# Attention block: query and key biases moved into the projection weights, and VectorE's work of a unit put in another order

## The chip, the cores and the metric

The kernel runs on one NeuronCore of a Trainium2 chip. Five engines work side by side, each on its own queue and in that queue's order: TensorE (PE in the profile; its weight loads are shown as PEld), VectorE (DVE), ScalarE (ACT), GpSimd (POOL), and SyncE (SP), which here only starts DMA transfers. The metric is the device time of one execution in microseconds (us). Before the change three runs took 2816.67, 2817.36 and 2818.38 us; the median is 2817.36 us.

## The reference, cut to what matters

Four sequences of 1024 tokens with 512 features go through a layer norm, a two-branch attention with 16 heads of 128, and a small fp8-rounded product, all added to the input.

```python
xn = _layernorm(x)                                   # mean 0 over the 512 features
q  = apply_rope(rmsnorm(xn @ Wq  + bq,  qn_w), pos)  # 16 heads x 128
lk = apply_rope(rmsnorm(xn @ Wlk + blk, kn_w), pos)
lv = xn @ Wlv + blv
# branch 1: top 8 of the compressed keys (one entry for every 4 tokens)
# branch 2: softmax over a window of the previous and the current 128 tokens
out = merged @ Wo + bo
```

The two lines with `bq` and `blk` are what the change is about. Since `xn` has mean zero over the features, subtracting one and the same row from every row of a weight matrix leaves `xn @ W` as it is. With the first row subtracted, the first row of the new matrix is zero: feature 0 then contributes nothing, and its place can carry a bias, if the input's feature 0 is replaced by 1.

## The kernel before, in words

The work is cut into 32 chunks of 128 tokens (`t`, eight for each of four sequences; `c` is the chunk's place in its sequence) and, within a chunk, into eight units of two heads (`u`), so 256 units `n = 8 t + u`. One long loop (line 791) runs over `s`; in one pass it issues parts of several units, so that the stages of different units overlap. What each engine does in which order is exactly the order of the calls in this loop; nothing reorders it later.

In one pass before the change, for `8 <= s`:

1. `scores(s)` (TensorE, L572 to L583), `keep_context(s-2)` (ScalarE), `weigh(s)` (VectorE L605 to L611: mask, maximum, top 8; ScalarE: the exponentials, L612 and L620), `queries(s+3)` (TensorE, L445 and L446), `settle(s)` (VectorE L627 to L638: sums, reciprocals, scaling).
2. one step of the chunk's preparation, then `squares(s+3)` (ScalarE, L296) and `spread(s+3)` (GpSimd, L290 and L291: the reciprocal root `r`), `settle_window(s)` (ScalarE, L643), `to_output(s-2)` (TensorE, L753), another step.
3. `turn(s)` (VectorE transposes the probabilities, L661; SP writes them to DRAM, L669), `values_of(s+1)` (TensorE, L537), `normalize(s+3)` (VectorE L467 and, in `rotate`, GpSimd L309 beside VectorE L310, then VectorE L311 and L312, which wait for L309), `values(s-1)` (TensorE, L720), `fetch(s)` (SP reads the probabilities back, L703), `turn_keys(s+3)` and `fetch_keys(s+3)` (VectorE L512 and L515; SP L520 and L530), `keep_values(s+1)` (ScalarE).

In the first chunk the turned keys and probabilities don't go through DRAM: TensorE transposes them (`turn_keys_here`, L490; `turn_here`, L684) and ScalarE and VectorE copy the results (`keep_keys`, `keep_turned`). In the first four units VectorE and GpSimd also round a weight matrix (`round_w2`, by `quantize`, L262 to L273).

`queries` makes 128 x 512 products: four float32 matmuls over the 512 features and a fifth, L446, which adds the bias: its weights are a column of `sel` repeated, its moving operand `bias_b`, three bfloat16 pieces of the bias.

`chunk_prep` is a generator that prepares a chunk two chunks ahead in steps ("A0", "B0", ...), two steps a pass: statistics (L329), the normalised rows `xn` (L337, VectorE), their transposes (L342), the copy `xnT` (L345, ScalarE), the compressed keys and values. For the first chunk it runs at once, at the start.

PSUM tiles: `qp` and `sc` have two buffers each, `pp` (transposes, `vp` and the chunk's products) has two, `ctx` one.

Of the kernel before, what the change touches and what calls it, by code (L numbers as in the profile page):

```python
# [23 lines left out]
HALF = ROPE // 2  # L24
# [14 lines left out]
def kernel(  # L39
# [46 lines left out]
    def scratch(name, shape=(P, 512), dtype=F32):  # L86
        return work.tile(list(shape), dtype, tag="scratch", name=name, bufs=2)
# [8 lines left out]
    x_tiles, angles = {}, {}  # L96
# [148 lines left out]
    def late_constants():  # L245
# [6 lines left out]
        nc.tensor.transpose(bp[:, 0:NH], blv_n, ident[:NH, :NH])  # L252
        nc.scalar.activation(blvT, bp[:, 0:NH], AF.Copy, scale=0.5)

    def quantize(dst, src, scalar, tag, m=None):

        v = scratch(f"qv_{tag}") if tag[0] == "x" else src
        if m is None:  # L260
            m = scratch(f"qm_{tag}")
        nc.vector.tensor_scalar(v, src, scalar, None, ALU.mult)  # L262
        nc.vector.tensor_scalar(
            m.bitcast(U32), v.bitcast(U32), 0x7F800000, None, ALU.bitwise_and
        )
        nc.vector.tensor_scalar(m, m, FP8_MIN_NORMAL, 1.5 * 2.0**20, ALU.max, ALU.mult)
        nc.gpsimd.tensor_tensor(v, v, m, ALU.add)
        yield
        nc.gpsimd.tensor_tensor(v, v, m, ALU.subtract)
# [3 lines left out]
        nc.gpsimd.tensor_tensor(dst, v, m, ALU.add)  # L273
        yield
# [22 lines left out]

    def rotate(th, cs, nh, a, name):

        p = th.shape[0]  # L300
        a = a.rearrange("p (h t f) -> p h t f", h=nh, t=2)
        bb = work.tile([P, 4, 2, HALF], F32, tag="ropeb", name=f"rb_{name}", bufs=1)
        bb = bb[:p, 0:nh]
        x12 = th[:, :, 0:ROPE].rearrange("p h (t f) -> p h t f", t=2)

        def wide(v):
            return v.unsqueeze(1).unsqueeze(1).to_broadcast([p, nh, 2, HALF])

        nc.gpsimd.tensor_tensor(bb, x12, wide(cs[:, HALF:ROPE]), ALU.mult)  # L309
        nc.vector.tensor_tensor(a, x12, wide(cs[:, 0:HALF]), ALU.mult)  # L310
        nc.vector.tensor_tensor(x12[:, :, 0, :], a[:, :, 0, :], bb[:, :, 1, :], ALU.subtract)  # L311
        nc.vector.tensor_tensor(x12[:, :, 1, :], a[:, :, 1, :], bb[:, :, 0, :], ALU.add)  # L312

# [4 lines left out]
    def chunk_prep(t):  # L318
# [14 lines left out]
        if c == 0:  # L333
            nc.gpsimd.memset(cv, 0.0)
        yield "B0"
        xn = scratch(f"xn_{t}")
        nc.vector.tensor_scalar(xn, xt, st[:, 6:7], r, ALU.subtract, ALU.mult)  # L337
        yield "A1"
        yield "B1"
        xp = pp(f"xp_{t}")  # L340
        for k in range(KK):
            nc.tensor.transpose(xp[:, ts(k, P)], xn[:, ts(k, P)], ident)  # L342
        yield "A2"
        xnT = work.tile([P, KK, P], F32, tag="xnT", name=f"xnT_{t}")
# [55 lines left out]
        er = rstd_of(ess, 1, 1.0 / D, EPS_RMS, f"er_{t}")  # L400
        ck = kv[:, 0:1, :]
        yield "A6"
        yield "B6"
        nc.vector.scalar_tensor_tensor(
            ck[:, 0, :], ck[:, 0, :], er, norm_w[0:NE, 1, :], ALU.mult, ALU.mult
        )
        ra = work.tile([NE, ROPE], F32, tag="ra_e", name=f"ra_e{t}", bufs=1)
        rotate(ck, angles[t][1], 1, ra, f"e{t}")
        yield "A7"
        yield "B7"  # L410
        cp = pp(f"cp_{t}")
        nc.tensor.transpose(cp[:, 0:NE], ck[:, 0, :], ident[:NE, :NE])
        yield "A8"
        nc.vector.tensor_copy(ckT[:, ts(c, NE)], cp[:, 0:NE])  # L414
        yield "B8"

    def chunk_eight(t):

        xt, xnT = x_tiles["sum", t], chunks[t]
        x8 = work.tile([P, KK * P], BF16, tag="x8", name=f"x8_{t}", bufs=1)  # L420
        src = xnT.rearrange("p k s -> p (k s)")
# [14 lines left out]
    def place(n):  # L436

        return divmod(n, NU)

    def queries(n):  # L440
        t, u = place(n)
        xnT = chunks[t]
        qp = psum.tile([P, 512], F32, tag="qp", name=f"qp_{n}")
        for k in range(KK):
            nc.tensor.matmul(qp, xnT[:, k, :], wqk_sb[u][:, k, :], start=(k == 0), stop=False)  # L445
        nc.tensor.matmul(  # L446
            qp, sel[:, u : u + 1].to_broadcast([P, P]), bias_b, start=False, stop=True
        )
# [10 lines left out]
        w["r"] = rstd_of(w["ss"], 4, 1.0 / D, EPS_RMS, f"r_{n}")  # L459

    def normalize(n):
        t, u = place(n)
        w = units[n]
        qp, r = w.pop("qp"), w["r"]
        th = work.tile([P, 4, D], F32, tag="th", name=f"th_{n}", bufs=1)
        for i in range(4):
            nc.vector.scalar_tensor_tensor(  # L467
                th[:, i, :],
                qp[:, ts(i, D)],
                r[:, i : i + 1],  # L470
                norm_w[:, i // 2, :],
                ALU.mult,
                ALU.mult,
            )
        thb = work.tile([P, NB, 2, 2 * BLK], F32, tag="thb", name=f"thb_{n}", bufs=1)
        spare = thb.rearrange("p b t x -> p (b t x)")[:, 0 : 4 * ROPE]
        rotate(th, angles[t][0], 4, spare, f"{n}")
        w["th"], w["thb"] = th, thb

    def by_dma(n):  # L480

        return NU <= n < NN - 1
# [308 lines left out]
    for s in range(-3, NN + 2):  # L791
        t, u = place(s)

        if s == -2 or u == 7 and 0 <= t and t + 2 < NT:
            running = [*running[-2:], chunk_prep(t + 2)]
        if u == 3 and 0 <= t < NT:
            load_x(t, "sum")
        if u == 6 and 0 <= t < NT:
            running = [*running[-2:], chunk_eight(t)]
        if u == 4 and 0 <= t and t + 2 < NT:  # L800
            load_x(t + 2, "norm")

        for_unit(s, (scores, 0), (scores, 1))
        for_unit(s - 2, (keep_context,))
        for_unit(s, (weigh, 0), (weigh, 1))
        for_unit(s + 3, (queries,))
        if s + 2 < NU:
            for_unit(s + 2, (turn_keys_here,))
        for_unit(s, (settle, 0), (settle, 1))
        if s < 0:  # L810
            until(first, ("B3", "B4", "B6")[s + 3])
        steps()
        for_unit(s + 3, (squares, (0, 1, 2, 3)), (spread,))
        if s + 2 < NU:
            for_unit(s + 2, (keep_keys,))
        for_unit(s, (settle_window, 0), (settle_window, 1))
        for_unit(s - 2, (to_output,))
        steps()
        if by_dma(s):
            turn(s)  # L820
        if s == -1:
            until(first, "B7")
        for_unit(s + 1, (values_of,))
        if s == -1:
            until(first, "B8")
        if not by_dma(s):
            for_unit(s, (turn_here,))
        for_unit(s + 3, (normalize,))
        for_unit(s - 1, (values,))
        if by_dma(s):  # L830
            fetch(s)
        else:
            for_unit(s, (keep_turned,))
        if s + 3 >= NU:
            for_unit(s + 3, (turn_keys,), (fetch_keys,))
        for_unit(s + 1, (keep_values,))
        if s < NU:
# [63 lines left out]
```

## Time and profile before

| | before |
|---|---|
| median of three runs | 2817.36 us |
| the profiled execution | 2818.54 us |
| its span | 2816.8 us |
| granted TensorE clock | 0.998 |
| TensorE busy | 2779.5 us |
| VectorE busy | 2244.6 us |
| ScalarE busy | 1282.1 us |
| GpSimd busy | 815.2 us |
| L446 (the bias matmul) | 256 times, 97.0 us busy |

The span runs from the first to the last instruction of one profiled execution. Busy time is the time in which an engine had at least one instruction in it. Matmuls are pipelined: the next one starts while the last is still draining, so the time from one start to the next, and not the mean duration of a row, is what a matmul takes from TensorE.

### The profile page before, as it was taken

Reading aid. Unit: us, or ns where it says so; the run is one execution under the profiler, and the core shown is the slowest. Engines: PE = TensorE matmul, PEld = TensorE weight load, DVE = VectorE, ACT = ScalarE, POOL = GpSimd, SP = SyncE. Lnnn points to the kernel's source line nnn. Section 1 sums busy time; section 2 is a strip of 40 time slices with the busy share of each in tenths; the row PEclk is TensorE's granted clock in tenths of the full one; section 3 lists DMA queues with packets and bytes.
Section 4 is the critical chain, followed back from the end, with each engine's and each line's share of the span. In section 5 each row is a group of like instructions: output and inputs, shape, how many; then the busy total and the mean of one; then the engine's idle time right before and its main releaser. Section 6 shows DMA issues by size and latency. Waiting matters only on the chain.

```text
span 2816.8 us, 48762 instructions
## 1 busy us (share of the span) xinstructions
PE 2779.5 (99%) x12969; PEld 1873.5 (67%) x12969; DVE 2244.6 (80%) x9132; ACT 1282.1 (46%) x5075; POOL 815.2 (29%) x1161
## 2 busy tenths in 40 slices
PE   6999999999999999999999999999999999999998
PEld 4666666666666666666666666666666666666665
DVE  5777888888777788888877777888887777788886
ACT  3445444444444444444444444444444444444443
POOL 3432222222333222322233333223222332322221
PEclk9999999999999999999999999999999999999999
DMA  7345455555445455555544454555554454455554
GB/s 231 91 136 141 134 143 150 148 154 150 130 124 139 137 140 144 148 152 149 155 127 127 134 136 134 154 150 148 145 154 121 134 134 135 133 158 156 145 145 114
DMA packets 620852, 399.85 MB, mean 142 GB/s; under 512 B 306881, under 2 KB 573985, under 8 KB 620577
## 3 DMA queue, kind: packets, MB, share of 16 engines
q1 hardware_dynamic: 608352, 383.18, 49.3%
q10 hardware_dynamic: 12224, 13.56, 1.6%
q8 instruction: 105, 1.72, 0.3%
q14 instruction: 171, 1.39, 0.2%
HBM read 212.53 MB, written 184.03 MB: 141 GB/s over the span
## 4 chain that ended last, share of the span: by engine, by line
PE 92%; DVE 3%; DMA 1%; POOL 1%; ACT 1%; SPq 0%; issue 0%; ACTq 0%; DVEq 0%; POOLq 0%
PE qp L445 30%; PE op L753 15%; PE vp L537 15%; PE cp L720 13%; PE sc L582 5%; PE sc L572 4%; PE sc L579 4%; PE qp L446 2%; PE yp L352 2%; PE fp L425 1%; DMA pr<-probB 1%; PE ep L382 1%; PE xp L342 0%; DMA probT<-pr 0%; ACT junk L296 0%
## 5 line engine op out<-in xcount | busy, mean ns | idle before, releaser
L445 PE MATMUL qp<-wqk,xnT 128*128 128x512 f32 x2048 | 944.6, 604 | 4.6 <-DMA scales<-in_L_ffn_scale_dram 3.3
L612 ACT ACTIVATE prob<-sc,neg 128x256 f32<-128x256 f32 (+1 forms) x512 | 236.1, 461 | 1029.6 <-DVE taken L611 975.9
L445 PEld LDWEIGHTS qp<-wqk,xnT 128*128 128x128 f32 x2048 | 370.3, 191 | 384.2 <-issue 370.5
L537 PEld LDWEIGHTS vp<-wlv,xnT 128*128 128x128 f32 x2048 | 388.8, 190 | 166.9 <-issue 113.1
L537 PE MATMUL vp<-wlv,xnT 128*128 128x256 f32 x2048 | 484.2, 379 | 4.8 <-DVE lkT L497 3.0
L753 PE MATMUL op<-wo,cT 128*128 128x512 f32 x1024 | 488.0, 599 | 0.5 <-ACT cT L735 0.5
L467 DVE SCALAR_TENSOR_TENSOR th<-qp,r,norm_w 128x128 f32<-128x128 f32 x1024 | 283.2, 339 | 104.8 <-POOL r L291 104.8
L661 DVE STREAM_TRANSPOSE probB<-prob 128x512 f32<-128x512 f32 (+2 forms) x494 | 283.1, 611 | 92.8 <-ACT prob L643 81.5
L290 POOL TENSOR_SCALAR r<-ss 128x4 f32<-128x4 f32 x256 | 49.9, 195 | 1038.5 <-ACT junk L296 1032.9
L309 POOL TENSOR_TENSOR rb<-th,cs 128x256 f32<-128x256 f32 x256 | 245.3, 958 | 269.4 <-DVE th L467 268.3
L296 ACT ACTIVATE junk<-qp 128x128 bf16<-128x128 f32 x1024 | 284.2, 278 | 54.8 <-PE qp L446 26.5
L720 PE MATMUL cp<-probT,lv 128*128 128x128 f32 x1920 | 299.3, 276 | 6.6 <-DMA probT<-pr 6.5
L753 PEld LDWEIGHTS op<-wo,cT 128*128 128x128 f32 x1024 | 186.4, 190 | 177.9 <-issue 120.5
L720 PEld LDWEIGHTS cp<-probT,lv 128*128 128x128 f32 x1920 | 274.4, 192 | 23.3 <-issue 10.0
L291 POOL TENSOR_TENSOR r<-r,nhalf 128x4 f32<-128x4 f32 x256 | 259.2, 1012 | 21.4
L720 PE MATMUL cp<-probT,cv 128*128 128x128 f32 x1536 | 256.1, 276 | 0.0
L582 PE MATMUL sc<-ckT,qT 128*128 128x96 f32 (+7 forms) x1024 | 227.1, 304 | 0.7 <-DVE ckT L414 0.7
L643 ACT ACTIVATE prob<-prob,tot 128x256 f32<-128x256 f32 (+1 forms) x512 | 223.2, 484 | 3.2 <-DVE tot L637 3.2
L549 ACT COPY lv<-vp 128x256 f32<-128x256 f32 x256 | 94.9, 371 | 276.2 <-PE cp L720 241.6
L720 PEld LDWEIGHTS cp<-probT,cv 128*128 128x128 f32 x1536 | 213.5, 193 | 0.0
L311 DVE TENSOR_TENSOR th<-thb,rb 128x128 f32<-128x128 f32 x256 | 87.2, 341 | 155.7 <-POOL rb L309 155.0
L605 DVE CUSTOM_DVE_ANT_0 sc<-sc,mask_b 128x256 f32<-128x256 f32 (+1 forms) x512 | 202.8, 396 | 8.3 <-PE sc L583 7.7
(123 smaller groups left out, 4054.0 us busy)
## 6 DMA issues: line engine op xcount, KB each, us to landing
pr<-probB SPq DMA_DIRECT2D x127, 512.0 KB, 3.0
probT<-pr SPq DMA_DIRECT2D x508, 128.0 KB, 2.9
qk<-thb SPq DMA_DIRECT2D x992, 64.0 KB, 2.0
pr<-probB SPq DMA_DIRECT2D x96, 384.0 KB, 2.8
probT<-pr SPq DMA_DIRECT2D x384, 96.0 KB, 2.4
qT<-qk SPq DMA_DIRECT2D x248, 128.0 KB, 2.3
lkT<-qk SPq DMA_DIRECT2D x248, 128.0 KB, 2.6
x_norm<-_attn_hidden_states_dram SPq DMA_DIRECT2D x32, 256.0 KB, 3.3
```

The source lines that it names most:

```text
L291: nc.gpsimd.tensor_tensor(r, r, nhalf[: ss.shape[0], 0:n], ALU.pow)
L296: nc.scalar.activation(junk[: src.shape[0]], src, AF.Square, accum_out=acc)
L309: nc.gpsimd.tensor_tensor(bb, x12, wide(cs[:, HALF:ROPE]), ALU.mult)
L445: nc.tensor.matmul(qp, xnT[:, k, :], wqk_sb[u][:, k, :], start=(k == 0), stop=False)
L467: nc.vector.scalar_tensor_tensor(th[:, i, :], qp[:, ts(i, D)], r[:, i : i + 1], norm_w[:, i // 2, :], ALU.mult, ALU.mult,)
L537: nc.tensor.matmul(vp[:, 0:256], xnT[:, k, :], wlv_sb[u][:, k, :], start=(k == 0), stop=(k == KK - 1),)
L582: nc.tensor.matmul(sc[:, spa], q, ckT[:, 0:m], start=True, stop=False)
L612: nc.scalar.activation(prob[:, loc], sc[:, loc], AF.Exp, bias=neg[:, 0:1], scale=-1.0, accum_out=tot[:, 0:1],)
L643: nc.scalar.mul(prob[:, loc], prob[:, loc], tot[:, 0:1])
L661: nc.vector.transpose(pb[:, :, ds(h * g, g), :], prob[:, parts[0] * P : (parts[-1] + 1) * P].rearrange("p (g b i) -> p b g i", b=NB, i=BLK),)
L720: nc.tensor.matmul(blocks(cp[:, h, :]), v, probT[:, :, h * len(parts) + i - parts[0], :], start=(i == parts[0]), stop=(i == parts[-1]),)
L753: nc.tensor.matmul(op, cT[:, h, :], wo_sb[u][:, h, :], start=(u == 0 and h == 0), stop=(u == NU - 1 and h == 1),)
```

## The change

- **Bias.** From the second chunk on, L446 is left out. Instead `xnT` has a fifth block of 128 features: a copy of the first block with its first row set to 1 (one more ScalarE copy and a VectorE memset for each chunk but the first), and `queries` uses this block in place of the first. The weights for it are made during the first chunk: in pass `s` (0 to 7) VectorE subtracts the first row from all of `wqk[s]` (128 x 2048 float32 elements), and SP's queue then writes the two bias pieces over its first row. The row comes to all partitions by two DMAs on SP's queue, one pass ahead. The first chunk itself still uses L446.
- **Mean.** So that `xn` has a mean of zero to rounding, the mean is taken out twice: GpSimd negates it, ScalarE subtracts it in place and sums the result, GpSimd scales that sum, and VectorE's `xn` subtracts the rest. `xn` comes one step later in `chunk_prep`; two of the later steps are joined, so that the generator has one pair of steps less.
- **Order.** `settle_window(s)` comes ahead of `squares(s+3)` on ScalarE. VectorE's `normalize` runs in pass `s` for unit `s+2` instead of `s+3`, ahead of `turn(s)`; its last two operations (`end_rotation`) come after `turn(s)` and the chunk's steps; `turn_keys(s+2)` follows there, so its four DMAs stand ahead of `fetch(s)` on SP's queue, and `fetch_keys(s+2)` behind it. In the first chunk `turn_keys_here` and `keep_keys` work on unit `s+1` instead of `s+2`. `rotate`'s GpSimd product has a buffer of its own for the units and one for the compressed keys.

```diff
+    def load_first_row(u):
+        row = work.tile([P, 1024], F32, tag="probB", name=f"first_row_{u}", bufs=1)[:, 0:512]
+        for i, w in enumerate((Wq, Wlk)):
+            nc.sync.dma_start(row[:, ts(i, 256)], w[0, ts(u, 256)].partition_broadcast(P))
+        first_row[u] = row
+    def fold_first_row(u):
+        w = wqk_sb[u]
+        nc.vector.tensor_tensor(
+            w, w, first_row.pop(u).unsqueeze(1).to_broadcast([P, KK, 512]), ALU.subtract
+        )
+        for i, bias in enumerate((bq, blk)):
+            nc.sync.dma_start(
+                w[0:1, 0, ts(i, 256)], bias[ts(u, 256)].partition_broadcast(1)
+            )
...
         nc.vector.tensor_tensor(a, x12, wide(cs[:, 0:HALF]), ALU.mult)
+        yield
         nc.vector.tensor_tensor(x12[:, :, 0, :], a[:, :, 0, :], bb[:, :, 1, :], ALU.subtract)
...
+        nc.gpsimd.tensor_scalar(off[:, 0:1], st[:, 6:7], -1.0, None, ALU.mult)
+        nc.scalar.activation(
+            xt, xt, AF.Identity, bias=off[:, 0:1], scale=1.0, accum_out=off[:, 1:2]
+        )
+        nc.gpsimd.tensor_scalar(off[:, 1:2], off[:, 1:2], 1.0 / HID, None, ALU.mult)
...
-        nc.vector.tensor_scalar(xn, xt, st[:, 6:7], r, ALU.subtract, ALU.mult)
+        nc.vector.tensor_scalar(xn, xt, off[:, 1:2], r, ALU.subtract, ALU.mult)
...
+        if t:
+            nc.scalar.copy(xnT[:, KK, :], xp[:, 0:P])
+            nc.vector.memset(xnT[0:1, KK, :], 1.0)
...
         for k in range(KK):
-            nc.tensor.matmul(qp, xnT[:, k, :], wqk_sb[u][:, k, :], start=(k == 0), stop=False)
-        nc.tensor.matmul(
-            qp, sel[:, u : u + 1].to_broadcast([P, P]), bias_b, start=False, stop=True
-        )
+            nc.tensor.matmul(
+                qp,
+                xnT[:, k if k or not t else KK, :],
+                wqk_sb[u][:, k, :],
+                start=(k == 0),
+                stop=(t > 0 and k == KK - 1),
+            )
+        if not t:
+            nc.tensor.matmul(
+                qp, sel[:, u : u + 1].to_broadcast([P, P]), bias_b, start=False, stop=True
+            )
...
         for_unit(s + 3, (queries,))
-        if s + 2 < NU:
-            for_unit(s + 2, (turn_keys_here,))
+        if s + 1 < NU:
+            for_unit(s + 1, (turn_keys_here,))
         for_unit(s, (settle, 0), (settle, 1))
+        for_unit(s, (settle_window, 0), (settle_window, 1))
+        for_unit(s + 2, (normalize,))
+        if by_dma(s):
+            turn(s)
...
         for_unit(s + 3, (squares, (0, 1, 2, 3)), (spread,))
...
         steps()
-        if by_dma(s):
-            turn(s)
+        for_unit(s + 2, (end_rotation,))
+        if s + 2 >= NU:
+            for_unit(s + 2, (turn_keys,))
...
-        for_unit(s + 3, (normalize,))
         for_unit(s - 1, (values,))
         if by_dma(s):
             fetch(s)
...
-        if s + 3 >= NU:
-            for_unit(s + 3, (turn_keys,), (fetch_keys,))
+        if s + 2 >= NU:
+            for_unit(s + 2, (fetch_keys,))
         for_unit(s + 1, (keep_values,))
+        if 0 <= s < NU:
+            fold_first_row(s)
+        if 0 <= s + 1 < NU:
+            load_first_row(s + 1)
```

More of the change, by code (lines that the diff above doesn't have):

```diff
@@ L253, in late_constants @@
         nc.scalar.activation(blvT, bp[:, 0:NH], AF.Copy, scale=0.5)
+    first_row = {}
+    def load_first_row(u):
[12 more added lines that the diff above has]
+            )
     def quantize(dst, src, scalar, tag, m=None):
@@ L301, in rotate @@
         a = a.rearrange("p (h t f) -> p h t f", h=nh, t=2)
-        bb = work.tile([P, 4, 2, HALF], F32, tag="ropeb", name=f"rb_{name}", bufs=1)
-        bb = bb[:p, 0:nh]
+        bb = work.tile([p, nh, 2, HALF], F32, tag=f"ropeb{nh}", name=f"rb_{name}", bufs=1)
         x12 = th[:, :, 0:ROPE].rearrange("p h (t f) -> p h t f", t=2)
@@ L335, in chunk_prep @@
         yield "B0"
+        off = work.tile([P, 2], F32, tag="off", name=f"off_{t}")
+        nc.gpsimd.tensor_scalar(off[:, 0:1], st[:, 6:7], -1.0, None, ALU.mult)
[3 more added lines that the diff above has]
+        nc.gpsimd.tensor_scalar(off[:, 1:2], off[:, 1:2], 1.0 / HID, None, ALU.mult)
+        yield "A1"
         xn = scratch(f"xn_{t}")
-        nc.vector.tensor_scalar(xn, xt, st[:, 6:7], r, ALU.subtract, ALU.mult)
-        yield "A1"
+        nc.vector.tensor_scalar(xn, xt, off[:, 1:2], r, ALU.subtract, ALU.mult)
         yield "B1"
@@ L343, in chunk_prep @@
         yield "A2"
-        xnT = work.tile([P, KK, P], F32, tag="xnT", name=f"xnT_{t}")
-        nc.scalar.copy(xnT.rearrange("p k s -> p (k s)"), xp)
+        xnT = work.tile([P, KK + 1, P], F32, tag="xnT", name=f"xnT_{t}")
+        nc.scalar.copy(xnT[:, 0:KK, :].rearrange("p k s -> p (k s)"), xp)
+        if t:
+            nc.scalar.copy(xnT[:, KK, :], xp[:, 0:P])
+            nc.vector.memset(xnT[0:1, KK, :], 1.0)
         chunks[t] = xnT
@@ L402, in chunk_prep @@
         yield "A6"
-        yield "B6"
         nc.vector.scalar_tensor_tensor(
@@ L407, in chunk_prep @@
         ra = work.tile([NE, ROPE], F32, tag="ra_e", name=f"ra_e{t}", bufs=1)
-        rotate(ck, angles[t][1], 1, ra, f"e{t}")
-        yield "A7"
-        yield "B7"
+        for _ in rotate(ck, angles[t][1], 1, ra, f"e{t}"):
+            pass
+        yield "B6"
         cp = pp(f"cp_{t}")
         nc.tensor.transpose(cp[:, 0:NE], ck[:, 0, :], ident[:NE, :NE])
-        yield "A8"
+        yield "A7"
         nc.vector.tensor_copy(ckT[:, ts(c, NE)], cp[:, 0:NE])
-        yield "B8"
+        yield "B7"
     def chunk_eight(t):
@@ L420, in chunk_eight @@
         x8 = work.tile([P, KK * P], BF16, tag="x8", name=f"x8_{t}", bufs=1)
-        src = xnT.rearrange("p k s -> p (k s)")
+        src = xnT[:, 0:KK, :].rearrange("p k s -> p (k s)")
         yield from quantize(x8, src, scales[:, 0:1], f"x_{t}")
@@ L461, in normalize @@
     def normalize(n):
-        t, u = place(n)
         w = units[n]
@@ L476, in normalize, with end_rotation @@
         spare = thb.rearrange("p b t x -> p (b t x)")[:, 0 : 4 * ROPE]
-        rotate(th, angles[t][0], 4, spare, f"{n}")
+        w["rotation"] = rotate(th, angles[place(n)[0]][0], 4, spare, f"{n}")
+        next(w["rotation"])
         w["th"], w["thb"] = th, thb
+    def end_rotation(n):
+        for _ in units[n].pop("rotation"):
+            pass
     def by_dma(n):
@@ L813 @@
         for_unit(s + 3, (squares, (0, 1, 2, 3)), (spread,))
-        if s + 2 < NU:
-            for_unit(s + 2, (keep_keys,))
-        for_unit(s, (settle_window, 0), (settle_window, 1))
+        if s + 1 < NU:
+            for_unit(s + 1, (keep_keys,))
         for_unit(s - 2, (to_output,))
         steps()
-        if by_dma(s):
-            turn(s)
+        for_unit(s + 2, (end_rotation,))
+        if s + 2 >= NU:
+            for_unit(s + 2, (turn_keys,))
         if s == -1:
@@ L823 @@
         for_unit(s + 1, (values_of,))
-        if s == -1:
-            until(first, "B8")
         if not by_dma(s):
             for_unit(s, (turn_here,))
-        for_unit(s + 3, (normalize,))
         for_unit(s - 1, (values,))
```

## The prediction, written before the result

> **What bounds the kernel.** I read the page's head first: who is busy, and what the chain that ended last consists of.
>
> ```profile
> span 2816.8 us, 48762 instructions
> ...
> PE 2779.5 (99%) x12969; PEld 1873.5 (67%) x12969; DVE 2244.6 (80%) x9132; ACT 1282.1 (46%) x5075; POOL 815.2 (29%) x1161
> ...
> PE 92%; DVE 3%; DMA 1%; POOL 1%; ACT 1%; SPq 0%; issue 0%; ACTq 0%; DVEq 0%; POOLq 0%
> ```
>
> TensorE is busy 99% and makes 92% of the chain. A busy share can hide waits, so I checked it in the timeline of TensorE for one unit of a late chunk (columns: start, length, engine, line, operation).
>
> ```profile
> 1405.55 3.68 PE L445 MATMUL qp<-wqk,xnT 128*128 128x512 f32 x8
> 1409.07 0.38 PE L446 MATMUL qp<-bias_b,sel 128*128 128x512 bf16 x1
> 1409.28 1.88 PE L753 MATMUL op<-wo,cT 128*128 128x512 f32 x4
> 1411.00 1.89 PE L537 MATMUL vp<-wlv,xnT 128*128 128x256 f32 x8
> 1412.73 0.61 PE L720 MATMUL cp<-probT,lv 128*128 128x128 f32 x4
> ```
>
> Starts follow each other without a hole; the unit's `scores` start at 1403.59 and those of the next at 1414.51, a period of 10.92 us filled with matmuls. TensorE is the bound from about 100 us to about 2770 us. Next VectorE, the nearest rival, by its waits (who waited for whom: us in total, times, longest):
>
> ```profile
> DVE th L311 <- POOL rb L309: 155.0, 250, 0.6
> DVE th L467 <- POOL r L291: 104.8, 82, 3.2
> DVE probB L661 <- ACT prob L643: 81.5, 96, 2.3
> DVE logits L363 <- ACT y L361: 48.7, 31, 5.3
> ```
>
> These are holes in VectorE's queue, not in TensorE's. In the last chunk of a sequence (window 1315 to 1407) VectorE is busy 77.6 of 92.0 us, waits 10.8 us, and has 3.6 us of small gaps.
>
> **The bias matmul goes.** 256 L446 less the 8 of the first chunk are 248. Its row says 379 ns, but in the timeline the next matmul starts 0.215 us after it (1409.07 to 1409.28). By the row's mean I would save 94 us, by the pitch 248 x 0.215 = 53.3 us. Here the Trainium skill speaks against the change: "TensorE: Matmul & The Clock Gate", section Back-to-back issue gap, gives 131 ns for 512-column matmuls in a sustained stream with weight loads, and says that the isolated 216 ns over-counts. By that the saving is 32.5 us. The measured pitch decides: 53.3 us. Nothing is left exposed by the removal: L753's first weight load would run beside the last L445 matmul, as the first load of L537 runs beside the last of L753, at the full pitch (four matmuls in 1.72 us). TensorE gets no other work.
>
> **The fold in the first chunk.** Eight VectorE subtractions of 128 x 2048. Two nearby rows of the same kind: L310, 256 elements, 0.43 us, and L197, 512 elements, 0.68 us; that is 1.0 ns an element, so 0.43 + 1792 x 0.001 = 2.2 us each, 18 us in all. The cover is whatever VectorE has free there. The unit rate of VectorE's `weigh` in units 0 to 4 is 41.76 to 85.51, 10.9 us a unit, while TensorE needs 9.87. One unit of VectorE after the change, from the timeline around 63.8 to 73: `weigh` and `settle` 5.3, normalise 1.55, `lkT` 0.35, chunk steps 0.5, rotation 0.5, `probT` 0.35, fold 2.2, rounding 1.35: 12.1 us. That is 1.2 us over before in units 0 to 3, so 4.8 us; in units 4 to 7 the rounding and the slow rows below go, 8.8 us, and TensorE's 9.87 leads again.
>
> The lock on the SBUF port belongs here. Rows, VectorE then GpSimd:
>
> ```profile
> 65.50 1.10 DVE L627 SCALAR_TENSOR_TENSOR prob<-taken,prob 128x32 f32<-128x32 bf16 x1
> 67.45 1.22 DVE L636 TENSOR_SCALAR tot<-tot 128x2 f32<-128x2 f32 x1
> ...
> 65.29 1.27 POOL L269 TENSOR_TENSOR wo<-wo 128x512 f32<-128x512 f32 x1
> 67.37 1.28 POOL L273 TENSOR_TENSOR w_sb<-wo 128x512 bf16<-128x512 f32 x1
> ```
>
> L627 takes 0.19 us elsewhere in this chunk and L636 0.17; here each ends with the GpSimd row. The Trainium skill, "SBUF — State Buffer", section SBUF: two separate sides, has the rule: a VectorE operation with two SBUF inputs, or in its two-port mode, and a GpSimd operation exclude each other for the whole instruction. By the rows I keep the 2.0 us a unit in the 5.3 above and add nothing for the fold. By the rule the fold, with two SBUF inputs, can also be held by GpSimd's root L291 (1.01 us) in each of eight units, 8 us more. I take nothing, since L291 follows `squares` and is over when `probT` is copied, and keep 8 us for the range.
>
> Against this, two terms at the start. The first chunk's `xn` now waits for ScalarE's mean pass. ScalarE stands in DMA issues until 9.12 and its table load ends at 10.40; then mean pass 0.8 (row L345's 0.59 plus a 0.19 accumulator read), GpSimd 0.2, `xn` 0.55, transposes 1.1, copy 0.6 and the small gaps between: first `queries` at 13.9 instead of 11.06, +2.9 us. The second `queries` waited for its weights until 19.89 anyway (1.3 us), and the old waits of TensorE for `th` (2.2 and 2.0 us, L490) go, since the first keys are turned a pass later behind three `queries` in a row. Followed through, the first `scores` come at 38.1 instead of 38.7. VectorE's first `weigh`, at 41.76 before because `normalize` and `ckT` stood ahead, starts near 39, a reserve that I don't count. 4.8 less 0.6 gives +4 us for start and first chunk together, which I take; from both sides, -3 (the start's gain alone) to +13 (with the lock).
>
> SP's queue in this chunk gains 32 DMAs (two rows, two biases a unit). They wait for the fold; behind them stand x loads and, in passes 6 and 7, the key transfers of units 8 and 9, which are issued before that pass's fold. The biases are needed five passes later. Nothing.
>
> **Per chunk, 31 or 32 times.** ScalarE: 0.8 for the mean and about 0.3 (L735's 128 x 128 form is 0.37) for the extra copy, 35 us on an engine busy 46%. GpSimd: two of 0.19 us. VectorE: a memset, 0.1 (L176 is 0.09), and one wait for the mean: ScalarE must wait for GpSimd's L309 ahead of it, 0.7 us a chunk. The cover is VectorE's slack below; without it each would cost TensorE its length, 25 us. ckT is done a pass earlier, so TensorE's wait for it (0.7 us in three places) goes.
>
> **The order in a pass.** In time from W, the start of `weigh(s)`, in a late chunk: `weigh` to 2.9, `settle` to 5.2, normalise and L310 to 6.7, `turn` to 7.9, rotation to 8.4, key transposes to 9.1; L309 (0.96, about 0.55 of it after L310) is over near 7.3, under `turn`, so the 0.62 us wait of L311 goes. The root `r` now has a whole pass, so most of the 104.8 goes; `settle_window` ahead of `squares` is done at 5.6, so the 81.5 goes. VectorE then needs 77.6 + 0.1 + 3.6 + about 2 of new waits = 83 us for that chunk against TensorE's 92.0 - 8 x 0.215 = 90.3. It stays covered. `queries(s+4)` needs `normalize(s+2)` out of PSUM: at W + 6.3, some 5 us early.
>
> What is late next is the probabilities' way through DRAM. SP: write at 7.9, the four key writes wait for 9.1 and take 1.9, the fetch then issues from 11.0; the last of four starts 1.3 later and lands 2.9 later: W + 15.2. Before, the fetch stood ahead of the keys. `values(s)` starts on TensorE 10.7 + 8.9 after `scores(s)`, W + 18.6. 3.4 us of slack, less chunk steps (0.9 on average, 2.1 seen) and VectorE's lag. Before, that slack was 2.5 with a lag of 2.6. Nothing.
>
> The tail has no `queries`, and keeps its DMA waits (3.7 and 1.2 us): 0, from -3 to +3.
>
> **Sum.** 2818.5 (the profiled execution: span 2816.8 and 1.7 around it) - 53.3 + 4 = 2769.2. The median lies 1.2 below that execution: **2768**.
>
> **Rivals.**
> - *VectorE takes over* (chance 0.16). If the new order keeps its waits (10.8 us in a late chunk), VectorE needs 92 us there against TensorE's 90.3, and the chunks from c = 5 on gain nothing: 53.3 x 20/32 = 33 saved, 2788. For it: 155 us of waiting on GpSimd, whose work isn't reduced. Against: those waits have another operation put into them.
> - *The DRAM way decides* (0.07), the slower side. From `scores(s)` through fetch and `values(s)` to `scores(s+2)`: 1.0 + 15.2 + 1.8 = 18.0 us for two units, 9.0 a unit. TensorE's old pace of 10.92 is reached when it lengthens by 3.8 us. A landing of 4.2 (the longest fetch seen) instead of 2.9, steps of 2.1, and a lock of 1.3 before the rotation give 4.7: 11.35 a unit. If that held in the 160 units with c >= 3: +0.43 x 160 = 69, less 53.3 x 3/8 = 20, +4: 2870. Against: it needs all three in every unit.
> - *The saving isn't there* (0.03): if the slot is weight-load time in disguise (0.19 us a load), 0.025 x 248 = 6 us are left, less 4: 2815.
>
> **Numbers.** The forecast holds 0.74, with 2760 to 2780 of its own. The range 2759 to 2794 adds half of the first rival and the first-chunk bounds. Under 0.2% (5.6 us) a measurement can't tell a change from none. Faster: the forecast and 0.15 of the first rival's 0.16, 0.89; same: the third rival, 0.03; slower: the second rival and the first's rest (waits that lengthen), 0.08.
>
> **What would show it.** L446's successor: 8 bias matmuls left. TensorE's unit period in late chunks 10.70 instead of 10.92. No wait of L311's successor on GpSimd; VectorE's `weigh` starting within 1.5 us of its scores. In the first chunk eight rows of 2.2 us and a unit rate near 12. Wrong would be: waits of `cp` on `probT` in the hundreds of us, or a VectorE share above 90%.

## The result, and the profile after

The changed kernel took **2799.16 us** (median of 4 runs, 2798.13 to 2802.21) against 2817.10 of the kernel before beside it: ratio 0.9938, 95% interval 0.9923 to 0.9953. It is faster, by 0.6%, where 1.7% were forecast; 2799 lies above the range that the prediction gave. The profiled execution has a span of 2796.6 us.

The head of the profile after (busy time and share of each engine, then the chain that ended last):

```profile
span 2796.6 us, 48466 instructions
...
PE 2735.4 (98%) x12721; PEld 1856.4 (66%) x12721; DVE 2263.3 (81%) x9171; ACT 1345.1 (48%) x5170; POOL 842.6 (30%) x1225
...
PE 92%; DVE 2%; DMA 1%; issue 0%; SPq 0%; ACT 0%; POOL 0%; DVEq 0%; ACTq 0%; POOLq 0%
```

TensorE was busy 44.1 us less, 2735.4 against 2779.5, yet the span shrank by 20.2 only. Its idle time rose from 37 to 61 us, so the rest is to be looked for in holes. (The 44.1 are less than the 53.3 forecast because the matmuls of the first chunk took longer, by 8.7 us in sum; the last section has the lines.) The same unit of a late chunk as was shown of before, in TensorE's timeline (start, length, engine, line):

```profile
1404.63 0.40 PE L616 MATMUL sc<-lkT,qT 128*128 128x128 f32 x2
...
1406.59 3.68 PE L478 MATMUL qp<-wqk,xnT 128*128 128x512 f32 x8
1410.10 1.88 PE L797 MATMUL op<-wo,cT 128*128 128x512 f32 x4
1411.82 1.89 PE L581 MATMUL vp<-wlv,xnT 128*128 128x256 f32 x8
...
1415.33 0.40 PE L616 MATMUL sc<-lkT,qT 128*128 128x128 f32 x2
```

No bias matmul stands between L478 and L797, and the unit has gone from 10.92 to 10.70 us: no hole here. VectorE's three largest waits over the whole run (us in total, times, longest):

```profile
DVE sc L649 <- PE sc L627: 279.6, 175, 3.1
DVE kv L335 <- POOL rb_e L332: 37.6, 32, 1.2
DVE probT L736 <- ACT probT L736: 20.5, 6, 5.7
```

The 155 us on GpSimd's rotation product, the 105 on the root and the 82 on ScalarE's `prob` are gone: of the rotation only that of the compressed keys is left (37.6), and in the whole run L506 (L467 before) idles 5.7 us and L705 (L661 before) not at all. VectorE now waits for TensorE's scores, which is slack. In a late chunk (1300 to 1392) it is busy 78.8 us and waits 7.9 for scores.

The loss is ahead of all this. I cut each timeline at one matmul, `scores`' product with `ckT` (L626 here), in units 0, 8 and 16; it starts 0.3 to 0.6 us after the first matmul of `scores` of which the prediction speaks. "Chunk 0" is from unit 0 to unit 8.

| kernel | median us | ratio to before (95%) | unit 0 starts | chunk 0 | chunk 1 | unit 8 to the end |
|---|---|---|---|---|---|---|
| before | 2817.10 | | 39.3 | 83.4 | 83.4 | 2694.1 |
| the change | 2799.16 | 0.9938 (0.9923 to 0.9953) | 44.6 | 113.7 | 83.6 | 2638.3 |

From unit 8 on the change gains 55.8 us. Ahead of it, 5.3 are lost at the start and 30.3 in chunk 0. The chain of waits inside chunk 0 (start, length, what) says how a unit went there:

```profile
131.15 0.36 ACT junk L318 x2
...
132.33 0.37 ACT junk L318 x2
132.70 0.29 ACT qT L540
133.01 0.43 DVE lkT L541
133.49 1.99 PE vp L581 x8
135.48 0.44 PE tp L728 x4
135.92 0.91 PE cp L764 x8
136.85 0.38 ACT probT L736
137.29 0.31 issue
137.60 2.28 DVE wqk L269
139.88 0.21 DVE sc L649
```

Three engines take turns, one step at a time: `squares` and `qT` on ScalarE, `lkT` on VectorE, `vp`, `tp` and `cp` on TensorE, `probT` on ScalarE, then VectorE's fold (L269), and only then the next unit's mask (L649), `settle`, and `squares` again. The unit takes 12 us though no engine has 12 us of work (VectorE is busy 10.1 us and TensorE 9.9 between 136 and 148; the line stands in the last section). I call that a ring: each engine waits for the one before it.

### The profile page after: what moved, and what is told of

Read it like the earlier page. It is cut to its first block, busy times and chain, and to the rows that moved or that the text cites. A ratio compares the mean times of both kernels' runs of the same rounds, so it can differ in the third digit from the quotient of the medians.

```text
span 2796.6 us, 48466 instructions
## 1 busy us (share of the span) xinstructions
PE 2735.4 (98%) x12721; PEld 1856.4 (66%) x12721; DVE 2263.3 (81%) x9171; ACT 1345.1 (48%) x5170; POOL 842.6 (30%) x1225
## 4 chain that ended last, share of the span: by engine, by line
PE 92%; DVE 2%; DMA 1%; issue 0%; SPq 0%; ACT 0%; POOL 0%; DVEq 0%; ACTq 0%; POOLq 0%
PE qp L478 30%; PE op L797 15%; PE vp L581 15%; PE cp L764 14%; PE sc L626 5%; PE sc L616 4%; PE sc L623 4%; PE yp L386 2%; PE fp L458 1%; PE ep L416 1%; PE xp L373 0%; DVE wqk L269 0%; DMA probT<-pr 0%; PE sc L627 0%; DVE th L506 0%
## 5 line engine op out<-in xcount | busy, mean ns | idle before, releaser
L478 PE MATMUL qp<-wqk,xnT 128*128 128x512 f32 x2048 | 944.7, 604 | 2.8 <-issue 2.1
L478 PEld LDWEIGHTS qp<-wqk,xnT 128*128 128x128 f32 x2048 | 370.3, 191 | 382.9 <-issue 371.7
L581 PEld LDWEIGHTS vp<-wlv,xnT 128*128 128x128 f32 x2048 | 393.0, 192 | 181.6 <-issue 115.8
L581 PE MATMUL vp<-wlv,xnT 128*128 128x256 f32 x2048 | 490.9, 383 | 17.9 <-DVE lkT L541 13.6
L797 PE MATMUL op<-wo,cT 128*128 128x512 f32 x1024 | 488.0, 599 | 0.5 <-ACT cT L779 0.5
L649 DVE CUSTOM_DVE_ANT_0 sc<-sc,mask_b 128x256 f32<-128x256 f32 (+1 forms) x512 | 208.0, 406 | 279.8 <-PE sc L627 279.6
L687 ACT ACTIVATE prob<-prob,tot 128x256 f32<-128x256 f32 (+1 forms) x512 | 252.4, 493 | 129.1 <-DVE tot L681 127.8
L797 PEld LDWEIGHTS op<-wo,cT 128*128 128x128 f32 x1024 | 186.4, 190 | 189.4 <-issue 129.2
L506 DVE SCALAR_TENSOR_TENSOR th<-qp,r,norm_w 128x128 f32<-128x128 f32 x1024 | 286.8, 343 | 5.7 <-ACT junk L318 3.2
L705 DVE STREAM_TRANSPOSE probB<-prob 128x512 f32<-128x512 f32 (+2 forms) x494 | 281.9, 608 | 0.0
L626 PE MATMUL sc<-ckT,qT 128*128 128x96 f32 (+7 forms) x1024 | 226.3, 303 | 0.0
L623 PE MATMUL sc<-lkT,qT 128*128 128x128 f32 x1024 | 207.9, 285 | 0.0
L779 ACT ACTIVATE cT<-cp,blvT 128x128 f32<-128x128 f32 x512 | 160.0, 364 | 92.7 <-PE cp L764 83.4
```

What stands on the lines that cost most here:

```text
L478: nc.tensor.matmul(qp, xnT[:, k if k or not t else KK, :], wqk_sb[u][:, k, :], start=(k == 0), stop=(t > 0 and k == KK - 1),)
L506: nc.vector.scalar_tensor_tensor(th[:, i, :], qp[:, ts(i, D)], r[:, i : i + 1], norm_w[:, i // 2, :], ALU.mult, ALU.mult,)
L581: nc.tensor.matmul(vp[:, 0:256], xnT[:, k, :], wlv_sb[u][:, k, :], start=(k == 0), stop=(k == KK - 1),)
L623: nc.tensor.matmul(blocks(sc[:, P : 2 * P]), q, lkT[:, :, ds(h * BLK, BLK)], start=True, stop=True)
L626: nc.tensor.matmul(sc[:, spa], q, ckT[:, 0:m], start=True, stop=False)
L687: nc.scalar.mul(prob[:, loc], prob[:, loc], tot[:, 0:1])
```

## The experiments

Three theories. *Fold*: eight subtractions of 2.28 us on VectorE are the loss. *Order*: `settle_window` ahead of `squares`, and `lkT` behind `normalize`, close the ring above. *Start*: the mean passes make the first units late. Each ratio is to runs of the kernel before that stood beside it (medians 2814.8 to 2817.1 us). All stage figures are of one profiled execution of each kernel, cut as above. Two of these executions lie off their kernel's median, window_late's 4.5 us above and no_mean0's 3.8 below. The start of unit 0 scatters too: 44.6 to 45.7 in the change, no_fold, fold_moved and window_late, which run the same there.

| kernel | median us | ratio to before (95%) | unit 0 starts | chunk 0 | chunk 1 | unit 8 to the end |
|---|---|---|---|---|---|---|
| order_only | 2826.21 | 1.0037 (1.0023 to 1.0051) | 38.5 | 97.9 | 83.4 | 2688.6 |
| bias_only | 2868.86 | 1.0188 (1.0173 to 1.0203) | 45.1 | 104.5 | 84.2 | 2718.6 |
| no_fold | 2785.47 | 0.9890 (0.9876 to 0.9905) | 45.0 | 100.8 | 81.6 | 2637.5 |
| fold_moved | 2788.49 | 0.9901 (0.9887 to 0.9916) | 45.7 | 100.4 | 85.7 | 2641.6 |
| keys_first | 2782.69 | 0.9885 (0.9870 to 0.9900) | 43.8 | 98.7 | 83.0 | 2638.6 |
| window_late | 2792.25 | 0.9919 (0.9903 to 0.9936) | 45.6 | 111.0 | 83.6 | 2638.3 |
| no_mean0 | 2794.84 | 0.9925 (0.9911 to 0.9940) | 41.3 | 110.4 | 83.6 | 2637.6 |
| first_old | 2794.72 | 0.9927 (0.9912 to 0.9942) | 47.4 | 108.0 | 82.4 | 2638.8 |
| order_keys | 2811.66 | 0.9989 (0.9982 to 0.9996) | 40.2 | 83.6 | 83.4 | 2687.8 |
| best_a | 2775.61 | 0.9857 (0.9842 to 0.9872) | 40.3 | 92.7 | 86.4 | 2641.1 |
| best_b | 2772.73 | 0.9843 (0.9830 to 0.9857) | 39.3 | 93.4 | 83.0 | 2638.3 |
| floor | 2775.16 | 0.9856 (0.9842 to 0.9869) | 41.0 | 94.0 | 81.6 | 2638.8 |

### The two halves of the change by themselves

**order_only** keeps every bias matmul and leaves the fold, its row loads and the mean passes out:

```
-        if 0 <= s < NU:
-            fold_first_row(s)
-        if 0 <= s + 1 < NU:
-            load_first_row(s + 1)
...
-                stop=(t > 0 and k == KK - 1),
+                stop=False,
             )
-        if not t:
-            nc.tensor.matmul(
+        nc.tensor.matmul(
```

> The new order alone: every chunk keeps its bias matmul, and mean pass, extra xnT block, fold and first-row loads are left out. Figures are the start of unit 8's scores (122.2 before, 157.8 after) and the time (2817 before). Theory 'fold' (the eight subtractions of 2.28 us on VectorE are the loss): unit 8's scores at 118 to 126, since the order by itself costs nothing, and 2813 to 2821, with a unit period of 10.92 later on. Theory 'order' (settle_window ahead of squares makes qT late, lkT stands behind it and behind normalize, and TensorE waits): unit 8's scores at 132 to 142 without any fold, and 2827 to 2837. Theory 'start' (mean pass): first scores near 39, and no more loss than that.

The order alone costs 14.5 us in chunk 0 (97.9 less 83.4) with no fold in the kernel, and the kernel is slower than before. Unit 8's scores come at 136.4, where *order* had them; the time is 0.8 us below its range. TensorE's waits between 40 and 160 us:

```profile
PE vp L571 <- ACT xnT L370: 4.4, 1, 4.4
PE tp L718 <- DVE lkT L531: 4.1, 3, 2.3
PE vp L571 <- DVE lkT L531: 3.1, 1, 3.1
PE vp L571 <- DVE total L411: 2.4, 1, 2.4
```

They add up to 14.0 us; before has 4.0 there. (The other 4.5 us of the 14.5 are longer matmuls: TensorE is busy 83.9 us in this chunk where it was 79.5 before.) `vp` and `tp` need one of the two `pp` buffers, which `lkT` and the chunk's steps behind it on VectorE set free. So the theory *order* holds for about half of the loss, and *fold* alone falls.

**bias_only** is the other half: the kernel before with mean pass, extra block, shortened `queries` and fold, in the old order.

```
+        if 0 <= s < NU:
+            fold_first_row(s)
+        if 0 <= s + 1 < NU:
+            load_first_row(s + 1)
```

> The bias in the weights' first row, mean pass, extra block and fold with the old order. Theory 'fold': the fold is on VectorE's path as before, eight times 2.3 to 3 us, so unit 8's scores at 140 to 150, and 2782 to 2792. Theory 'order': with the old order VectorE takes the fold at 1.2 us a unit in four units as the forecast had it, unit 8's scores at 126 to 132, and 2768 to 2774. If the new order is needed for the saving later on (rival 'VectorE takes over'), the unit period in late chunks stays above 10.8 and the time is 2790 or more.

A surprise: 1.9% slower than before, with 248 matmuls less. Unit 8 lies where *fold* had it, but the large part is in the later chunks, which should have gained 53 us and lost 24.5 (2718.6 against 2694.1). The last chunk of a sequence takes 93.0 to 93.1 us; with TensorE as the bound, as in the change, it takes 90. VectorE's waits over 93 us from there on, 1400 to 1493 (the last chunk of a sequence ends at 1468):

```profile
DVE th L329 <- POOL rb L327: 5.6, 9, 0.6
DVE th L501 <- POOL r L309: 3.0, 3, 1.6
DVE probB L695 <- ACT prob L677: 2.0, 3, 1.3
DVE logits L390 <- ACT y L388: 1.3, 1, 1.3
DVE xnT L372 <- ACT xnT L371: 1.3, 1, 1.3
DVE kv L329 <- POOL rb_e L327: 0.2, 1, 0.2
```

13.4 us of waits and 75.9 busy leave 3.7 of the 93 for small gaps. (In the last chunk itself, 1375 to 1468, the three are 12.0, 77.3 and 3.7.) None of these waits is for TensorE, so VectorE never runs out of work: it sets the pace. Before it was the same (77.6, 10.8 and 3.6 of 92.0). TensorE waits for VectorE's work instead, over the whole run of bias_only (the second line by way of the probabilities that VectorE turns and SP sends through DRAM):

```profile
PE sc L616 <- DVE ckT L441: 28.7, 24, 2.4
PE cp L754 <- DMA probT<-pr: 23.5, 30, 2.5
```

Before, these two waits were 0.7 and 6.5 us. Both engines stood at the bound, so work taken off TensorE alone brings nothing, and what the edit adds to VectorE is paid: the memset's wait for `xnT` (L372) alone is 38.5 us in the whole run. Which of the added pieces makes up the 24.5 was not separated. The order is what turns the edit into a gain.

### The fold

**no_fold** leaves out the subtraction and keeps its DMAs, so that the projection differs.

```
-        nc.vector.tensor_tensor(
-            w, w, first_row.pop(u).unsqueeze(1).to_broadcast([P, KK, 512]), ALU.subtract
-        )
```

> The changed kernel with only the VectorE subtraction of the fold left out (its DMAs stay; so the first row's bias is there but the row it replaces is not taken out of the others, which changes the projection). Theory 'fold': unit 8's scores at 122 to 130, and 2763 to 2771. Theory 'order': the ring keeps its waits, so unit 8's scores at 134 to 142, and 2776 to 2784. Of the start's 5.5 us neither removes anything.

The fold costs 12.9 us of chunk 0 (113.7 to 100.8). Unit 8's scores at 145.8 and the time, 2785.5, lie above both ranges, nearer to *order*. With 14.5 for the order, 2.9 of the 30.3 us are left for chunk 1's mean pass and the added DMAs. These three shares hold for this way of adding one piece after the other; the edits below, made in the full kernel, give others.

**fold_moved** puts the fold to where VectorE waits for the turned probabilities:

```
         for_unit(s + 2, (end_rotation,))
+        if 0 <= s < NU:
+            fold_first_row(s)
...
-        if 0 <= s < NU:
-            fold_first_row(s)
```

> The changed kernel with the fold issued between the end of the rotation and the copy of the turned probabilities, where VectorE waits 2.3 to 5.7 us in each unit of the first chunk, instead of at the end of the pass. Theory 'fold' (VectorE simply has too much to do): no gain, unit 8's scores at 154 to 158, 2796 to 2801. Theory 'order' (VectorE has waits beside the fold, in a ring): the fold fits into the wait, about 2.2 us in each of eight units less a lock, unit 8's scores at 138 to 146, and 2780 to 2788.

Chunk 0 is 100.4, as without any fold: there the 18 us of VectorE work cost nothing. VectorE had the time, at another place of its queue; but the time it used is a wait that the ring itself makes, and floor, below, shows what is left of the fold's cost without that wait. Unit 8's scores at 146.1 and the time lie at the upper edge of *order*'s ranges. Chunk 1 pays 2.1 us back, which best_b takes up.

### The order's parts

**keys_first** moves one step, for the first chunk's units only:

```
         for_unit(s, (settle, 0), (settle, 1))
+        if s + 1 < NU:
+            for_unit(s + 1, (keep_keys,))
         for_unit(s, (settle_window, 0), (settle_window, 1))
...
         for_unit(s + 3, (squares, (0, 1, 2, 3)), (spread,))
-        if s + 1 < NU:
-            for_unit(s + 1, (keep_keys,))
```

> The changed kernel with keep_keys (qT on ScalarE, lkT on VectorE) issued right after settle, ahead of settle_window and normalize, instead of after squares. Figures are the first chunk's length (first scores' ckT matmul of unit 0 to that of unit 8: 83.4 before, 113.7 after, 97.9 with the new order alone) and the time. Theory 'keys behind normalise' (TensorE's vp and tp wait for lkT, and lkT stands behind squares, qT and normalize): lkT comes some 2 to 3 us earlier in each unit, VectorE no longer waits for the turned probabilities, first chunk 94 to 102, time 2780 to 2788. Rival 'VectorE has too much to do': the unit stays at VectorE's own work, first chunk 108 to 114, 2794 to 2800.

Chunk 0 falls by 15.0 us and the kernel to 2782.7, inside the first theory's interval.

**order_keys** is order_only with this same diff:

> The new order alone (as the kernel with all bias matmuls kept and no fold), with keep_keys right behind settle. Theory 'keys behind normalise' explains the 14.5 us that the order alone cost in the first chunk (97.9 against 83.4): the first chunk falls to 83 to 87, first scores stay near 38.5, time 2812 to 2816, no slower than before. Rival 'settle_window and the later key transposes cost it by themselves': the first chunk stays at 92 or more, 2820 to 2826.

Chunk 0 is 83.6, that of before to 0.2 us, and the whole a little faster than before (0.9989, interval below 1). Unit 0 starts 1.6 us later than in order_only. So the order's whole cost in chunk 0 was the place of `keep_keys`: behind `settle_window` and `squares` on ScalarE, and behind `normalize` on VectorE. How much each of the three weighs was tested for the first alone:

**window_late** is that rival cause inside the order, `settle_window` back behind `keep_keys` while s < 8:

```
-        for_unit(s, (settle_window, 0), (settle_window, 1))
+        if s >= NU:
+            for_unit(s, (settle_window, 0), (settle_window, 1))
...
             for_unit(s + 1, (keep_keys,))
+        if s < NU:
+            for_unit(s, (settle_window, 0), (settle_window, 1))
```

> The changed kernel with settle_window behind squares and keep_keys in the first chunk, as before the change, instead of ahead of them. Theory 'settle_window makes qT late': squares and qT needn't wait for settle, about 1 us a unit, first chunk 104 to 108, time 2789 to 2794. Rival 'keys behind normalise': lkT waits on VectorE's normalize anyway, first chunk 111 to 114, 2796 to 2800.

Chunk 0, 111.0, is at the rival's end; the median, 2792.3, lies in the first theory's range. The profiled execution is the slowest of four, 4.5 us above the median, so that the 2.7 us it shows in chunk 0 may be too few; by the ratios the edit is worth some 5 us of the whole, with intervals that overlap. It isn't the main cause: keys_first takes out 15.0.

**first_old** keeps the old order up to pass 7, with the fold still at the end of a pass:

```
+        if s <= 7:
...
+            if s + 2 < NU:
+                for_unit(s + 2, (keep_keys,))
+            for_unit(s, (settle_window, 0), (settle_window, 1))
...
+            if s < 7:
+                for_unit(s + 3, (normalize,), (end_rotation,))
...
+        else:
```

> The changed kernel with the old order in passes -3 to 7 (settle_window late, keys turned two units ahead, normalize three ahead) and the new one from pass 8 on; mean pass, fold and its place at the end of the pass stay. The old order with the fold had a first chunk of 104.5. Theory 'order': first chunk 103 to 106, later chunks as in the changed kernel (2638 from unit 8 to the end), 2788 to 2792. Rival 'the fold alone': as the changed kernel, 2796 to 2800. A wait where the orders meet would show between units 8 and 10, 1 to 4 us.

A miss in part. Units 0 to 5 take 11.3 to 16.8 us, and where the orders meet TensorE waits 4.3 us for ScalarE's `settle_window` (unit 7 takes 15.6). Its start, 47.4, is the latest of all; I did not follow that up. The old order is no cure: the fold hurts there as well.

### The start

**no_mean0** leaves the mean pass out for chunk 0, which has its bias matmul anyway:

```
-        off = work.tile([P, 2], F32, tag="off", name=f"off_{t}")
...
+        if t:
+            off = work.tile([P, 2], F32, tag="off", name=f"off_{t}")
...
+        mean = off[:, 1:2] if t else st[:, 6:7]
```

> The changed kernel without the mean pass for chunk 0, which has its own bias matmul and the weights as loaded, so that the sum of the normalised row plays no part there; its xn is made from the mean of the statistics as before. Theory 'mean pass makes the start late': first scores at 38.3 to 39 instead of 44.3 (the new order alone had 38.5 for the ckT matmul), and 2791 to 2795. Rival 'the start is late since TensorE is at its low clock after any wait': the first scores come at 41 to 44, 2796 to 2799. The first chunk's length stays within 2 of 113.7 in both.

Between the two: unit 0 starts at 41.3, in the rival's range, and the time lies in the theory's; the ratio's interval overlaps the change's, so the gain in time is not clear of noise. In this execution 3.3 of the 5.3 us come back. ScalarE's timeline shows what kept the rest (start, length, engine, line; in brackets what ended the idle time before):

```profile
33.77 0.72 ACT L364 ACTIVATE x_norm<-x_norm,off 128x512 f32<-128x512 f32 x1 [1.93 <-POOL off L363]
34.40 0.18 ACT L364 ACTIVATION_READ_ACCUMULATOR x_norm<-x_norm,off 128x1 f32 x1
...
35.93 0.38 ACT L542 COPY qT<-tq 128x256 f32<-128x256 f32 x1
```

That is chunk 1's mean pass. It waits 1.93 us for GpSimd and stands ahead of unit 0's `squares` and `qT`; in order_only, which has no mean pass, `qT` starts at 33.54. TensorE's first `vp` waits 2.54 us for it by way of `lkT`. With `keep_keys` ahead of the chunk's steps as well, unit 0 starts at 40.3 (best_a) and 39.3 (best_b, as before the change). The rival has a part too: from 34.0 to 41.3 the granted clock was 0.50, and that `vp` took 3.78 us where it took 1.97 before. best_b's takes 3.78 as well, so the half clock is not what keeps no_mean0 behind best_b.

### Together

**best_a** has the three diffs of keys_first, fold_moved and no_mean0:

> The changed kernel with three edits together: keep_keys right behind settle, the fold between the end of the rotation and the copy of the turned probabilities, no mean pass for chunk 0. If the three losses are separate: first scores' ckT matmul at 37.5 to 40 (qT stands ahead of chunk 1's mean pass now), first chunk 98.7 less what of the fold then fits into VectorE's waits (8.7 us of waits for probT there), 90 to 95, the rest 2638.5: 2768 to 2774. If they are one loss told three times (the ring has one limit): first chunk stays at 97 to 100, 2776 to 2781.

Chunk 0 lies in the range given for separate losses; start and sum miss by 0.3 and 1.6 us, since chunk 1 grew to 86.4. Yet the three gains don't simply add up: alone they took 15.0, 13.3 and 3.3 us out of chunk 0, together 21.0 and not 31.6. In part it was one loss. TensorE at unit 9:

```profile
142.51 0.39 PE L766 MATMUL cp<-probT,cv 128*128 128x128 f32 x2
145.67 0.47 PE L618 MATMUL sc<-lkT,qT 128*128 128x128 f32 x2 [2.77 <-DMA qT<-qk]
```

On SP the key write of unit 9 (139.88) stood behind the bias DMAs (138.81), these behind the fold, and the fold behind its row, whose load stood behind the fetch of unit 8's keys. **best_b** mends that (its diff against best_a; `put_biases` holds the two bias DMAs that stood in `fold_first_row`):

```
-        if 0 <= s < NU:
-            fold_first_row(s)
         if s + 2 >= NU:
             for_unit(s + 2, (turn_keys,))
+        if 0 <= s < NU:
+            fold_first_row(s)
+            if s + 1 < NU:
+                load_first_row(s + 1)
...
-        if 0 <= s + 1 < NU:
-            load_first_row(s + 1)
+        if 0 <= s < NU:
+            put_biases(s)
+        if s == -1:
+            load_first_row(0)
```

> The three-edit kernel (keys first, fold moved, no mean pass for chunk 0), with SP's order mended: the next first row is loaded right behind the fold instead of behind the key fetch, the two bias DMAs go to the end of the pass behind the key fetch, and the fold itself comes after the keys' vector transposes. There a key write of unit 9 stood on SP behind the bias DMAs, which waited for a fold that waited 3.3 us for its row. Theory 'SP's order': TensorE's 2.8 us wait for the key fetch at unit 9 goes, chunk 1 falls from 86.4 to 82 to 83.5, time 2770 to 2773. Rival 'the wait only moves' (the fetch is late for another reason): chunk 1 at 85 or more, 2774 to 2777.

The wait went, chunk 1 is 83.0, and 2772.7 us is the fastest kernel of this study: 1.6% under before, and by the two ratios (0.9843 / 0.9938) 1.0% under the change. The intervals of best_a and best_b overlap; what the mended queue brings is read from the wait that went.

**floor** is best_b with no_fold's diff, so that its projection differs:

> The same as the mended three-edit kernel with the fold's VectorE subtraction left out (its DMAs stay; the row is not taken out of the weights, so the projection changes). It measures what the eight subtractions still cost there. If VectorE has room for them: first chunk within 3 us of the kernel with the fold, 2767 to 2772. If VectorE is full in units 0 to 3 as the forecast had it (1.2 us over the old unit in four units, 4.8, and more with the locks on GpSimd's rounding): first chunk 83 to 86, 6 to 10 us shorter, 2760 to 2766.

As a whole it tells nothing, and both its ranges are missed: in the profiled execution ScalarE took 11.0 us for its weight DMAs in unit 0 (44.28 to 55.31) where best_b took 5.2, and unit 0 alone lasted 21.2 us:

```profile
44.28 5.83 ACTq L898 DMA_DIRECT2D wo<-in_L_ffn_input_dram  x4
...
51.52 2.12 ACTq L128 DMA_DIRECT2D wlv<-in_L_attn_Wlv_dram  x1
53.69 1.62 ACTq L131 DMA_DIRECT2D wo<-in_L_attn_Wo_dram  x1
55.41 0.37 ACT L658 ACTIVATE prob<-sc,neg 128x128 f32<-128x128 f32 x1 [14.48 <-DMA wqk<-in_L_attn_Wq_dram]
```

Units 1 to 7 can be compared: 11.3, 9.9, 11.5, 9.9, 11.1, 9.6 and 9.4 us, against 14.4, 9.9, 16.7, 9.9, 13.0, 9.6 and 9.5 of best_b. So some 10 us of fold are left there, all in units 1, 3 and 5, in which a step of chunk 1 takes a `pp` buffer too (`yp`, `ep` and `cp`). What a fold spread over later passes would bring wasn't tried.

## Why the prediction was right and wrong

- **The bias matmul, −53.3 by the pitch: right.** From unit 8 to the end order_only has 2688.6 us and the change 2638.3: 50.3 less. The row's mean (94) is out, and so is what the Trainium skill's sustained figure ("TensorE: Matmul & The Clock Gate", section Back-to-back issue gap) would make of it, an estimate of 32.5.
- **The order in a pass: right, and needed more than I said.** L311's wait, the root's and `settle_window`'s went as forecast, the unit is 10.70, and `values` waits 5.7 us for the DRAM way in the whole run. The forecast for what happens otherwise (rival "VectorE takes over": 92 us in a late chunk) came true in bias_only, 93.0 to 93.1. Only, I costed that rival as a smaller gain, 2788; by itself it is a loss. (My window for the old last chunk, 1315 to 1407, began 20 us ahead of it; the chunk itself, 1334.9 to 1426.2, has 76.9 us busy, 10.8 of waits and 3.6 of gaps, which says the same.)
- **Start and first chunk together, +4 (−3 to +13): wrong.** It was +35.6, and this is the miss; the rest of the sum came out 2.5 us better than forecast (−55.8). Its terms:
  - *"One unit of VectorE after the change ... 12.1 us", then "TensorE's 9.87 leads again": the failing step.* I added VectorE's own durations, with `probT` following the rotation at once. Between `lkT` and `probT` stand `vp`, `tp` and `cp` on TensorE and a copy on ScalarE, and `lkT` itself had been moved behind `normalize` and, by way of `qT`, behind `settle_window` and `squares`. Units 0 to 3 took 13.8 to 18.4 us where I had 12.1, units 4 to 6 15.8, 12.0 and 11.9 where I had 9.87. order_keys shows the order's share (14.5 us, all of it from the place of `keep_keys`), no_fold the fold's (12.9), fold_moved that VectorE had time for the fold while the ring kept it waiting. The fold's term was too small besides: with the ring opened the eight folds still cost some 10 us (best_b against floor) where I had 4.8, all in three units with a chunk step that takes a `pp` buffer: 14.4, 16.7 and 13.0 us in best_b.
  - *The fold's length, 2.2 us: right* (median 2.28, once 2.81).
  - *The lock, 8 us in reserve: not taken, and turned round.* See the last section.
  - *"The first `scores` come at 38.1": wrong by 6.* First `queries` came at 14.14 (13.9 forecast). The cover failed. The second `queries` came right behind `yp` at 22.46, with no wait for weights left to hide in, and where TensorE's waits of 2.2 and 2.0 us for `tq` went, others of 4.60 (L445, for `kv`) and 2.54 (L581, for `lkT`) came. I left out that chunk 1's mean pass stands on ScalarE ahead of unit 0's `qT`; no_mean0 and best_b show that. The −0.6 that I had for mean pass and order together is what the order brings without the mean pass (order_only: −0.7).
- **SP's 32 added DMAs at nothing: nothing speaks against it in this kernel** (chunk 1 takes 83.6 us after 83.4, and TensorE has no wait for `qT` at unit 9), though no run takes them out alone; wrong as soon as the fold moves ahead of the key writes (best_a: a 2.8 us wait at unit 9).
- **The tail at 0: right within its bounds;** from unit 255's matmul to the end it is 21.9 us after 21.0.

With the ring opened and the start mended, best_b's 2772.7 lies within the forecast's own 2760 to 2780. Part of that is luck: chunk 0 still costs 10.0 us where start and chunk together were to cost 4, and the order gains 5.5 us from unit 8 on (2694.1 to 2688.6), for which I had no term.

## What to carry to other kernels

When an order is rewritten, follow one unit through all engines and not one engine through its own list: a step that is moved behind another is late by everything that stands between, and a fill stage with two buffers shows it where the steady state hides it. Before work is taken off the busiest engine, look at the waits of the second: if none of them is for the first, the second sets the pace as well, and the saving stays out until it is given slack. And look at the first chunk apart, since a loss of 30 us there disappears in busy shares of 98%.

## What the hardware did that I had not expected

**The port's lock goes to whoever starts first.** In the rows shown in the prediction VectorE waited for GpSimd. With the fold moved, GpSimd waited (best_b's timeline):

```profile
74.38 2.28 DVE L269 TENSOR_TENSOR wqk<-wqk,first_row 128x2048 f32<-128x2048 f32 x1
74.40 3.16 POOL L316 TENSOR_TENSOR r<-r,nhalf 128x4 f32<-128x4 f32 x1
```

The root began 0.02 us after the fold and took 3.16 us; in the change it takes 1.02 on average. "SBUF — State Buffer", section SBUF: two separate sides, of the Trainium skill says so: whichever starts first has the port pair for the whole instruction. I had read it in one direction.

**Waits of a few microseconds cost a second time through TensorE's clock.** The change's first chunk in windows cut near its units (busy time and instructions of each engine, then PEclk, DMA share and GB/s):

```profile
58.00:75.00 17.00, 11.71 (x49) 8.21 (x48) 11.80 (x39) 4.84 (x21) 6.67 (x8) 0.80 0.42 139
90.00:109.00 19.00, 14.69 (x54) 9.87 (x53) 11.90 (x37) 4.98 (x21) 6.59 (x7) 0.78 0.32 84
136.00:148.00 12.00, 9.94 (x49) 6.46 (x48) 10.10 (x34) 4.78 (x21) 2.02 (x2) 1.00 0.28 66
```

Where TensorE had waited, the granted clock was 0.78 to 0.80, and a `vp` of eight matmuls took 3.78 us instead of 1.89. Two of them in the change, and one of best_b (in brackets the wait ahead of each):

```profile
70.41 3.78 PE L581 MATMUL vp<-wlv,xnT 128*128 128x256 f32 x8 [5.29 <-DVE lkT L541]
102.84 3.78 PE L581 MATMUL vp<-wlv,xnT 128*128 128x256 f32 x8 [4.31 <-DVE total L420]
84.26 3.78 PE L586 MATMUL vp<-wlv,xnT 128*128 128x256 f32 x8 [2.79 <-DVE lkT L546]
```

"TensorE: Matmul & The Clock Gate", Part 1, of the Trainium skill has the rule: half clock after an idle window of about 3.4 us. The waits of 5.29 and 4.31 us agree. best_b's wait was 2.79 us, shorter than that window, and the granted clock behind it was 0.50 too (84.3 to 87.8); here the measurement decides.

How much of the 30 us is the clock's was not tested apart, but the windows from unit 0 to unit 8, of before and of the change, bound it:

```profile
39.26:122.70 83.44, 79.47 (x370) 52.49 (x370) 63.83 (x280) 37.99 (x167) 40.29 (x51) 0.98 0.48 146
44.59:158.26 113.67, 88.19 (x372) 59.40 (x371) 80.37 (x287) 39.32 (x171) 40.78 (x46) 0.89 0.43 124
```

For nearly the same matmuls TensorE was busy 8.7 us longer and idle 21.5 us longer. So at most some 8.7 of the 30.3 us are the slower clock's, and they are contained in the shares that the experiments gave to the order and to the fold.
